# Two attention layers on one core: the place of a pair's multiplication by its softmax reciprocals in the odd block

## The chip, the cores and the metric

The kernel runs on one core of one Trainium2 chip. The metric is the device time of one execution in microseconds (us); lower is better. A core has five engines that run beside each other, each with its own queue that is worked off strictly in the order written: TensorE (PE: matmuls), VectorE (DVE), ScalarE (ACT), GpSimd (POOL) and SyncE (SP). SP and POOL here mostly issue DMAs. Engines and DMAs wait for each other through semaphores.

## The reference

The input x has 16 images of 256 channels and 32x32 points (n = 1024), all float32. Two layers of the same form follow each other, each with its own weights:

```
xn   = group_norm(x)                      # 16 groups of the last axis, mean and variance over the rest
q, k, v = W xn + b                        # 256x256 each, split in 4 heads of 64
sim  = q^T k + rel^T q                    # per head, 1024x1024; rel = rel_h + rel_w
attn = softmax(sim)
x    = x + v attn^T
```

What matters here is the end of a head: the products of v with the unnormalised exponentials are multiplied by the reciprocal of the exponentials' sum, and the result, with the bias of v, is added to x (the residual).

## The kernel before, in words

**Work and order.** A unit is one layer of one image; there are 32, interleaved so that a layer-1 unit comes four or more units after its layer-0 unit. In a unit the four heads are taken as two pairs (`pr`), and each pair in two halves of 512 queries. This gives 4 blocks a unit and 128 blocks in all. Block n of a unit has the number b = n mod 4; blocks with b = 0 and 2 (half 0) are called even, those with b = 1 and 3 (half 1) odd. The order of all instructions is written out by hand (`tc.manual_schedule`): `block(n)` issues one block, and what each engine does follows the order of the lines there. Nothing is reordered.

**A block.** For each of 8 key tiles j: DVE seeds a PSUM tile with the position term (`seed`, L346), PE adds the scores (`scores`, L382, 8 instructions of 512 columns), ACT takes the exponential into a tile `p` (L391), and DVE adds the `p` tiles up in `acc` (`add_up`, L400 and L402). PSUM has room for four such tiles, named by a ring of four tags, so a seed must wait for the exponential (or other reader) that frees its tag. The first tile of the next block is seeded and scored within the block, the next three (`seed(after, j)` for j = 1 to 3) are seeded at its end. Then PE multiplies the exponentials by v (`attend`, L416) in two stretches of 64 instructions, and ACT copies the product from PSUM to `od` (`take_out`, L477).

**Pieces for later units.** Between the scores PE also does a projection, the values or the position terms of the next unit (L265, L295, L323). Odd blocks also average the group sums of the unit after next: DVE zeroes a small PSUM tile `pm` (L202), PE adds into it (L210, in two stretches), and ACT reads it out as `neg` (L220, b = 1) or `var` (L232, b = 3). `pm` sits under the tag that the seed of tile 1 of the next block takes next, so that seed waits for this read. Two stretches of matmuls on PE are kept in order by a tiny POOL memset, the token (L166): PE's second stretch waits for the token, and POOL writes it when its queue gets there and PE's first stretch is done.

**The sums of the exponentials.** They travel by DMA. POOL issues `acc<-p` (L433, adds the last tile), then a fold of `acc` in half (L438); SP stacks a quarter of it (L452) and POOL adds the other (L457). In the second block after a pair's last one, the odd block, POOL folds the stack five times (L462: 64, 32, 16, 8 and 4 rows), each fold waiting for the landing of the one before; the first four stand in POOL's queue ahead of the token for the second stretch of `attend`. SP spreads the result into `den_all` (L470). Late in the following even block DVE takes the reciprocals (L512), SP writes them to DRAM (L514, `rd<-r`) and reads them back, broadcast over 64 partitions each, into `rden` (L519). In SP's queue both stand behind that block's L452.

**The lines of this change.** In the odd block after that (two blocks behind the folds), `before` names the pair. `normalise` (L527) multiplies `od` by `rden` in place, one DVE instruction of 128x1024. `add_residual` (L534) adds `od` and the bias of v to x, again one DVE instruction of 128x1024, and in layer 1 has SP store x (L536). `finish` (L538) is the one followed by the other; the last unit's blocks without pieces call it already. On DVE the multiplication stands behind `add_up(previous, 6)` and ahead of `seed(blk, 4)`, the residual ahead of `seed(after, 1)`:

```
        for j in range(1, 4):
            scores(blk, j)
        if before:
            normalise(*before)
...
        add_up(blk, 5)
        if before:
            add_residual(*before)
```

Of the kernel before, what the change touches and what calls it, by code (L numbers as in the profile page):

```python
# [43 lines left out]
def flat(ap):  # L44
    return ap.rearrange("p w h -> p (w h)")
# [7 lines left out]
def fast_path(ctx, tc, sh, x, layers, out, W, den_all, token, good, flag):  # L53
# [140 lines left out]
    def norm_sums(u, gs):  # L194
        if u not in reds:
            reds[u] = small.tile([P, G], F32, tag="red", name=f"red_{u}")
        for g in gs:
            of_group(u, g, AF.Identity, reds[u])
# [159 lines left out]
    def widen(u, pr):  # L358

        r = W.rel[units[u][1]][:, pr, :]  # L360
        t = gnpool.tile([P, CC, N], F32, tag="gn", name=f"wide_{u}_{pr}")[:, 0, :]
        nc.vector.tensor_tensor(
            t.rearrange("p (w y) -> p w y", y=H),
            r[:, :H].unsqueeze(1).to_broadcast([P, sh.W, H]),
            r[:, H:].unsqueeze(2).to_broadcast([P, sh.W, H]),
            ALU.add,
        )
        wide[u, pr] = t

    def scores(blk, j, tag=None):  # L370

        u, pr, half = blk
        ps = psum2(tag, f"ps_{u}_{pr}_{half}_{j}") if tag else seeds.pop((blk, j))
        columns = slice(half * HALF, (half + 1) * HALF)
        for x, c in enumerate(QUARTERS):
            for h, hs in enumerate(QUARTERS):
                j0 = j * P + x * D
                terms = [(ks[u, pr], qs[u, pr])]
                if tag:
                    terms = [(qs[u, pr], wide[u, pr])] + terms  # L380
                for i, (a, b) in enumerate(terms):
                    nc.tensor.matmul(  # L382
                        ps[c, h, :],
                        a[hs, j0 : j0 + D],
                        b[hs, columns],
                        start=bool(tag) and i == 0,
                        stop=i == len(terms) - 1,
                        skip_group_check=True,
                    )
        p = ppool.tile([P, 2, HALF], F32, tag="p", name=f"p_{u}_{pr}_{half}_{j}")  # L390
        nc.scalar.activation(p, ps, AF.Exp, bias=W.shift)  # L391
        probs[blk, j] = p

    def add_up(blk, j):
        u, pr, half = blk
        if j == 0:
            return
        if j == 1:
            accs[blk] = apool.tile([P, 2, HALF], F32, tag="acc", name=f"acc_{u}_{pr}_{half}")
            nc.vector.tensor_tensor(accs[blk], probs[blk, 0], probs[blk, 1], ALU.add)  # L400
        else:
            nc.vector.tensor_tensor(accs[blk], accs[blk], probs[blk, j], ALU.add)  # L402
# [29 lines left out]
    def add_last(blk):  # L432
        nc.gpsimd.dma_start(accs[blk], probs[blk, NT - 1], accum_op=ALU.add)  # L433
# [25 lines left out]
    def fold_stack(u, pr, rows_):  # L459

        stack = stacks[u, pr]
        nc.gpsimd.dma_start(stack[:rows_], stack[rows_ : 2 * rows_], accum_op=ALU.add)  # L462
# [61 lines left out]
    def normalise(u, pr):  # L524
        o = outs[u, pr].rearrange("p x (k e) -> p x k e", e=8)
        rden = rdens.pop((u, pr)).rearrange("p (k x e) -> p x k e", x=2, e=8)
        nc.vector.tensor_tensor(o, o, rden, ALU.mult)  # L527

    def add_residual(u, pr):

        b, l = units[u]
        xs = xt[b][:, pr, :]
        o = outs.pop((u, pr)).rearrange("p a n -> p (a n)")
        nc.vector.scalar_tensor_tensor(xs, o, W.bv[l][:, pr : pr + 1], xs, ALU.add, ALU.add)  # L534
        if l == NL - 1:
            nc.sync.dma_start(flat(out[b, pr * P : (pr + 1) * P]), xs)  # L536

    def finish(u, pr):  # L538
        normalise(u, pr)
        add_residual(u, pr)  # L540
# [75 lines left out]
    def block(n):  # L616
        blk = blocks[n]
        u, b = divmod(n, BPU)
        pr_, half = blk[1:]

        stacked = blocks[n - 3][:2] if half == 1 and n > 2 else None
        summed = blocks[n - 4][:2] if half == 0 and n > 3 else None
        before = blocks[n - 5][:2] if half == 1 and n > 4 else None
        after = blocks[n + 1] if n + 1 < len(blocks) else None
        previous = blocks[n - 1] if n > 0 else None
        one, two = u + 1 < NU, u + 2 < NU

        pieces = u + 1 < NU or b < 2
        if u + 1 == NU and b == 1:
            widen(u, 1)  # L630
        f0, f1, f2, f3 = ring
        folded = n - 1 < FOLDED
        if not pieces:
            return block_without_pieces(n, half)

        if stacked:
            fold_stack(*stacked, D)
        if previous:
            add_up(previous, 6)
            if folded:  # L640
                add_last(previous)
            else:
                add_up(previous, 7)
        for j in range(1, 4):
            scores(blk, j)
        if before:
            normalise(*before)
        (first, first_out), (second, second_out) = prepare(u, b)
        first(0)
        if b == 0 and one:  # L650
            norm_apply(u + 1, range(0, 1))
        if b == 1 and two:
            norm_sums(u + 2, range(9, 11))
        seed(blk, 4, f1)
        scores(blk, 4)
        add_up(blk, 1)
        if b == 0 and one:
            norm_apply(u + 1, range(1, 5))
        if b == 1 and two:
            norm_sums(u + 2, range(11, 12))  # L660
        if b == 2 and two:
            norm_squares(u + 2, range(0, 5))
        second(0)
        if half == 1:
            second_out()
        first.word()
        if half == 0:
            second.word()
        if stacked:
            fold_stack(*stacked, R)  # L670
        if previous and folded:
            fold(previous)
        if stacked:
            fold_stack(*stacked, R // 2)
            fold_stack(*stacked, R // 4)
        first(1)
        first_out()
        seed(blk, 5, f0)
        scores(blk, 5)
        if previous and folded:  # L680
            stack_up(previous)
        add_up(blk, 2)
        if half == 0:
            second(1)
            second_out()
        seed(blk, 6, f1)
        scores(blk, 6)
        if half == 0:
            ring[2:] = f3, f2
        seed(blk, 7, ring[2])  # L690
        scores(blk, 7)
        add_up(blk, 3)
        add_up(blk, 4)
        if summed:
            reciprocals(*summed)

        if after:
            seed(after, 0, f0)
        if n in check:
            next(checks)  # L700
        if b == 0 and one:
            norm_apply(u + 1, range(5, 9))
        if b == 0 and two:
            norm_sums(u + 2, range(0, 2))
        if b == 1 and two:
            norm_sums(u + 2, range(12, G))
        if b == 1 and one:
            norm_apply(u + 1, range(9, 11))
        if b == 2 and two:
            norm_squares(u + 2, range(5, 11))  # L710
        po = psum2(ring[3], f"po_{n}")
        values_of_p = attend(blk, po)
        values_of_p(0)
        if two and half == 1:
            mean, mean_out = (norm_mean if b == 1 else norm_var)(u + 2, zeroed(f1, f"pm_{n}"))
            mean(0)
        if after:
            scores(after, 0)
        values_of_p.word()
        if two and half == 1:  # L720
            mean(1)
        if stacked:
            fold_stack(*stacked, R // 8)
            spread_sums(*stacked)
        if previous and folded:
            fold_again(previous)
        if half == 1 and u + 3 < NU and units[u + 3][1] == 0 and u > 0 or n == 3:
            load_x(units[u + 3][0], range(pr_, pr_ + 1) if u > 0 else range(CC))
        if two and half == 1:
            mean_out()  # L730
        add_up(blk, 5)
        if before:
            add_residual(*before)
        if after:
            for j in range(1, 4):
                seed(after, j, ring[j % 3])
        if b == 0 and two:
            norm_sums(u + 2, range(2, 9))
        if b == 1 and one:
            norm_apply(u + 1, range(11, G))  # L740
        if b == 2 and two:
            norm_squares(u + 2, range(11, G))
        values_of_p(1)
        take_out(blk, po)
        pos[n] = po
# [477 lines left out]
```

## Time and profile before

| | us |
|---|---|
| median of 7 runs | 2568.03 |
| lowest and highest run | 2564.18, 2576.93 |
| the profiled execution | 2573.06 |
| its span in the profile | 2571.3 |
| one multiplication L527 (63 of them) | 1.21 to 1.23 |
| one residual L534 (63 of them) | 1.27 to 1.29 |
| `acc<-p`, issue to landing (median) | 5.2 |
| `rd<-r`, issue to landing (median) | 1.6 |
| `rden<-rd`, issue to landing (median) | 4.0 |

In the profile, a row of the timeline gives the start from the span's beginning, the duration, engine, line and operation, output and inputs, the number of merged instructions, and in brackets the idle time of the engine ahead of it and who ended it. A row of the waits gives who waited for whom, the sum, the number of times and the longest. The profiler models the ends of matmuls, so a busy PE can hide short stalls; the starts of its rows show them. "+2.3" below means 2.3 us after the first score instruction of the block on PE (the row of 24 `L382` matmuls, tiles 1 to 3).

### The profile page before, as it was taken

How to read it: one execution, taken by the hardware profiler on the slowest of the kernel's cores; microseconds unless marked ns; L12 is line 12 of the kernel's file. 1: busy time of each engine (PE TensorE's matmuls, PEld its weight loads, DVE VectorE, ACT ScalarE, POOL GpSimd, SP SyncE). 2: the span in 40 equal slices, each digit the busy share in tenths (PEclk: the TensorE clock that was granted, in tenths of full speed). 3: DMA queues.
4: the chain of work that ended last, by engine and by line, in shares of the span. 5: the costliest groups of instructions: out<-in, count | busy, mean ns of one | idle time of the engine just before them, and what ended most of it. 6: DMA issues, size and time to landing. Idle time of an engine off the chain costs nothing. (4 is left out here: it accounts for less than half of the span.)

```text
span 2571.3 us, 86058 instructions
## 1 busy us (share of the span) xinstructions
PE 2533.3 (99%) x37474; PEld 1634.6 (64%) x37474; DVE 2254.3 (88%) x2076; ACT 1957.2 (76%) x3934; POOL 833.0 (32%) x1254
## 2 busy tenths in 40 slices
PE   8999999999999999999999999999999999999997
PEld 4666766766566665666666766666655677656664
DVE  6888898988888889889888888898888888989997
ACT  6778777787777887777877777877777777787753
POOL 1233333323333333333233333333333333323320
PEclk9999999999999999999999999999999999999999
DMA  3343443444444444444444444444444444443441
GB/s 89 72 79 75 85 86 74 92 95 91 86 98 99 81 82 92 88 92 84 95 83 86 99 87 78 93 96 88 83 92 98 84 80 88 74 84 76 86 91 57
DMA packets 119538, 221.06 MB, mean 86 GB/s; under 512 B 53736, under 2 KB 55272, under 8 KB 119152
## 3 DMA queue, kind: packets, MB, share of 16 engines
q0 software_dynamic: 53568, 129.58, 30.3%
q1 hardware_dynamic: 65584, 85.90, 11.9%
q8 instruction: 295, 4.83, 0.8%
q14 instruction: 91, 0.75, 0.1%
HBM read 51.78 MB, written 17.30 MB: 27 GB/s over the span
## 5 line engine op out<-in xcount | busy, mean ns | idle before, releaser
L346 DVE TENSOR_TENSOR ps<-abt 128x1024 f32<-128x1024 f32 x1018 | 1225.7, 1227 | 233.7 <-ACT p L391 56.4
L391 ACT ACTIVATE p<-ps,shift 128x1024 f32<-128x1024 f32 x1024 | 1092.9, 1114 | 356.4 <-PE ps L382 243.3
L382 PE MATMUL ps<-q,k 64*64 64x512 f32 x8192 | 1018.8, 592 | 12.6 <-DVE ps L346 11.5
L416 PE MATMUL po<-p,v 64*64 64x256 f32 x16384 | 941.6, 376 | 0.0
L416 PEld LDWEIGHTS po<-p,v 64*64 64x64 f32 x16384 | 779.1, 133 | 183.3 <-issue 45.2
L402 DVE TENSOR_TENSOR acc<-acc,p 128x1024 f32<-128x1024 f32 x644 | 783.5, 1217 | 4.9
L382 PEld LDWEIGHTS ps<-q,k 64*64 64x64 f32 x8192 | 374.5, 133 | 356.5 <-issue 182.7
L462 POOL DMA_DIRECT2D stack<-stack x310 | 251.6, 812 | 484.4 <-DMA stack<-stack 238.3
L166 POOL MEMSET token<- 1x1 f32 x380 | 40.6, 107 | 827.0 <-PE po L416 477.2
L295 PE MATMUL pv<-Wv,xn 64*64 64x256 f32 x4096 | 250.4, 377 | 0.5 <-DVE var L876 0.3
L265 PE MATMUL pq<-xn,Wq 64*64 64x512 f32 x2048 | 250.0, 593 | 0.3 <-DVE xn L908 0.3
L265 PE MATMUL pk<-xn,Wk 64*64 64x512 f32 x2048 | 248.4, 590 | 0.0
L457 POOL DMA_DIRECT2D stack<-acc x248 | 223.6, 1090 | 40.3 <-issue 30.6
L295 PEld LDWEIGHTS pv<-Wv,xn 64*64 64x64 f32 x4096 | 190.9, 134 | 67.5 <-issue 44.2
L245 ACT ACTIVATE xn<-x,nshift,rstd 128x128 f32<-128x128 f32 x496 | 211.2, 500 | 7.5 <-POOL nshift L236 7.5
L190 ACT ACTIVATE junk<-x,neg 128x128 f32<-128x128 f32 x498 | 195.3, 401 | 0.0
L438 POOL DMA_DIRECT2D acc<-acc x124 | 102.4, 826 | 233.0 <-DMA acc<-p 223.8
L265 PEld LDWEIGHTS pq<-xn,Wq 64*64 64x64 f32 x2048 | 100.6, 134 | 120.1 <-issue 113.0
L433 POOL DMA_DIRECT2D acc<-p x124 | 131.4, 1060 | 121.6 <-DVE acc L402 107.4
L265 PEld LDWEIGHTS pk<-xn,Wk 64*64 64x64 f32 x2048 | 95.5, 134 | 105.5 <-issue 105.5
L477 ACT COPY od<-po 128x512 f32<-128x512 f32 x127 | 74.4, 586 | 113.9 <-PE po L416 113.9
L400 DVE TENSOR_TENSOR acc<-p,p 128x1024 f32<-128x1024 f32 x128 | 155.7, 1217 | 0.0
(75 smaller groups left out, 1233.7 us busy)
## 6 DMA issues: line engine op xcount, KB each, us to landing
acc<-p POOLq DMA_DIRECT2D x124, 512.0 KB, 5.2
rden<-rd SPq DMA_DIRECT2D x126, 256.0 KB, 4.0
acc<-acc POOLq DMA_DIRECT2D x124, 256.0 KB, 3.4
x<-in_x_dram SPq DMA_DIRECT2D x32, 512.0 KB, 4.3
stack<-acc SPq DMA_DIRECT2D x248, 64.0 KB, 2.1
stack<-acc POOLq DMA_DIRECT2D x248, 64.0 KB, 3.2
out_dram<-x SPq DMA_DIRECT2D x31, 512.0 KB, 3.6
stack<-stack POOLq DMA_DIRECT2D x62, 128.0 KB, 2.7
```

Source lines behind the costliest of these rows:

```text
L190: nc.scalar.activation(junk, grouped(xt[units[u][0]], g), func, accum_out=into[:, g : g + 1], **bias)
L245: nc.scalar.activation(grouped(xns[u], g), grouped(xt[units[u][0]], g), AF.Identity, bias=shift[:, g : g + 1], scale=rstd[:, g : g + 1],)
L265: yield nc.tensor.matmul(pk[c, nh, :], w[l][rs, cc, c0 : c0 + D], xns[u][rs, cc, nh * HALF : (nh + 1) * HALF], start=(t == 0 and cc == 0), ...
L295: yield nc.tensor.matmul(pv[c, a, i, :], xns[u][rs, cc, j0 : j0 + D], W.wv[l][rs, cc, :], start=(t == 0 and cc == 0 and i == 0), stop=(t = ...
L346: nc.vector.tensor_tensor(ps.rearrange("p h (w y) -> p h w y", y=H), ab[:, :, :H].unsqueeze(2).to_broadcast([P, 2, XH, H]), ab[:, :, H + h ...
L382: nc.tensor.matmul(ps[c, h, :], a[hs, j0 : j0 + D], b[hs, columns], start=bool(tag) and i == 0, stop=i == len(terms) - 1, skip_group_check ...
L391: nc.scalar.activation(p, ps, AF.Exp, bias=W.shift)
L400: nc.vector.tensor_tensor(accs[blk], probs[blk, 0], probs[blk, 1], ALU.add)
L402: nc.vector.tensor_tensor(accs[blk], accs[blk], probs[blk, j], ALU.add)
L416: yield nc.tensor.matmul(po[c, a, :QUART], vts[u][rs, j, c0 : c0 + D], p[rs, h, a * QUART : (a + 1) * QUART], start=(t == 0 and j == 0), s ...
L457: nc.gpsimd.dma_start(at, acc[R:D, h, :], accum_op=ALU.add)
L462: nc.gpsimd.dma_start(stack[:rows_], stack[rows_ : 2 * rows_], accum_op=ALU.add)
```

## The change

The multiplication leaves the front of the odd block and is made directly in front of the addition, by calling `finish` where `add_residual` was called. It does so in 61 odd blocks (block 5 to block 125). On DVE the instruction moves behind the seeds of tiles 4 to 7, five additions, the seed of the next block's tile 0, the memset of `pm` and the sixth tile's addition, and stays ahead of the seeds of the next block's tiles 1 to 3. The residual now waits on the instruction in front of it. No instruction is added or removed, no DMA is moved, and the other engines' queues keep their order.

```
@@ -643,8 +643,6 @@
                 add_up(previous, 7)
         for j in range(1, 4):
             scores(blk, j)
-        if before:
-            normalise(*before)
         (first, first_out), (second, second_out) = prepare(u, b)
         first(0)
         if b == 0 and one:
@@ -730,7 +728,7 @@
             mean_out()
         add_up(blk, 5)
         if before:
-            add_residual(*before)
+            finish(*before)
         if after:
             for j in range(1, 4):
                 seed(after, j, ring[j % 3])
```

More of the change, by code (lines that the diff above doesn't have):

```diff
@@ L645, in block @@
             scores(blk, j)
-        if before:
-            normalise(*before)
         (first, first_out), (second, second_out) = prepare(u, b)
@@ L732, in block @@
         if before:
-            add_residual(*before)
+            finish(*before)
         if after:
```

## The prediction

> **What bounds the kernel now.** I read the page's totals and the costliest groups first, then who waits on VectorE (DVE), then TensorE's (PE's) rows block by block, and last the rows of DVE and GpSimd (POOL) around the multiplication. All times are microseconds of one profiled execution.
>
> ```profile
> PE 2533.3 (99%) x37474; PEld 1634.6 (64%) x37474; DVE 2254.3 (88%) x2076; ACT 1957.2 (76%) x3934; POOL 833.0 (32%) x1254
> ...
> PE po L416 8%; PE ps L382 8%; PE pq L265 2%; PE pv L295 2%; DVE ps L346 2%; PE pk L265 2%; DMA rden<-rd 1%; DVE acc L402 1%; DMA acc<-p 1%; DMA rd<-r 1%; PE pa L323 0%; DVE acc L400 0%; POOL rstd L234 0%; DMA stack<-acc 0%; DVE od L527 0%
> ```
>
> PE is the bound. In the chain that ended last (second line) its matmuls lead, and the transfer `rden<-rd` stands there beside DVE: it is what the multiplication (L527) waits for.
>
> ```profile
> DVE od L527 <- DMA rden<-rd: 53.5, 32, 4.2
> ...
> DVE ps L346 <- ACT var L232: 39.2, 30, 2.5
> DVE ps L346 <- ACT neg L220: 36.9, 30, 2.4
> ```
>
> These are DVE's waits (total, times, longest). In 32 of 63 cases the reciprocals land late and DVE stands idle, 1.7 each. The two lower rows are 60 idle times of 1.27 each, before the first of three seeds at the end of an odd block. That is the place to which the multiplication moves.
>
> A quiet odd block, PE, DVE and ACT rows:
>
> ```profile
> 1002.09 2.75 PE L382 MATMUL ps<-q,k 64*64 64x512 f32 x24
> 1002.81 1.23 DVE L527 TENSOR_TENSOR od<-od,rden 128x1024 f32<-128x1024 f32 x1 [0.42 <-DMA rden<-rd]
> 1004.34 1.23 DVE L346 TENSOR_TENSOR ps<-abt 128x1024 f32<-128x1024 f32 x1 [0.31 <-ACT p L391]
> ...
> 1015.84 1.27 DVE L534 SCALAR_TENSOR_TENSOR x<-od,bv,x 128x1024 f32<-128x1024 f32 x1
> ...
> 1018.15 0.18 ACT L220 ACTIVATE neg<-pm 128x16 f32<-128x16 f32 x1
> ...
> 1018.36 3.50 DVE L346 TENSOR_TENSOR ps<-abt 128x1024 f32<-128x1024 f32 x3 [1.25 <-ACT neg L220]
> ...
> 1020.34 2.81 PE L382 MATMUL ps<-q,k 64*64 64x512 f32 x24
> ```
>
> A disturbed one:
>
> ```profile
> 961.71 2.81 PE L382 MATMUL ps<-q,k 64*64 64x512 f32 x24
> ...
> 964.43 1.23 DVE L527 TENSOR_TENSOR od<-od,rden 128x1024 f32<-128x1024 f32 x1 [2.38 <-DMA rden<-rd]
> ...
> 965.58 1.23 DVE L346 TENSOR_TENSOR ps<-abt 128x1024 f32<-128x1024 f32 x1
> ...
> 966.86 1.09 PE L382 MATMUL ps<-q,k 64*64 64x512 f32 x8 [0.61 <-DVE ps L346]
> ...
> 979.43 3.61 DVE L346 TENSOR_TENSOR ps<-abt 128x1024 f32<-128x1024 f32 x3 [1.09 <-ACT var L232]
> ...
> 981.32 2.86 PE L382 MATMUL ps<-q,k 64*64 64x512 f32 x24
> ```
>
> A block begins with the PE row of 24 matmuls. The quiet block lasts 1020.34 - 1002.09 = 18.25; the next odd one, from 1040.98 to 1059.26, 18.28. The disturbed one lasts 19.61: DVE waited 2.38, the fifth seed (row 965.58) came at +3.87 instead of +2.25, and PE stood still for it. Even blocks last 20.6 to 20.7 nearly everywhere. So what can be won lies in odd blocks. Lengths read from PE's rows in this way, for the 60 odd blocks that begin from 131.86 to 2460, exceed the quiet length of their kind by 30.8 together, and the last one that the change touches (2499.18) by about 0.7: **31.5**. 25 blocks are long by over 0.1, 22 of them with `rden` late.
>
> **Part 1, what the front of the block loses.** 61 multiplications of 1.22 go from the front. In a quiet block this gives nothing: the fifth seed waits for the exponential of the second tile (`ACT p`, +2.25) with or without the multiplication ahead of it, and from there to the residual DVE runs without a gap. In a disturbed block the seed falls back to +2.25 and PE's stall there goes. Were that all, 31.5 less what has other causes would be won.
>
> **Part 2, what the end of the block gains.** The multiplication now runs from +13.75 (where the residual L534 stood). Three rows at the very end of the kernel show the same pair back to back, then an independent instruction:
>
> ```profile
> 2541.51 1.22 DVE L527 TENSOR_TENSOR od<-od,rden 128x1024 f32<-128x1024 f32 x1
> 2542.76 1.28 DVE L534 SCALAR_TENSOR_TENSOR x<-od,bv,x 128x1024 f32<-128x1024 f32 x1
> 2543.96 1.22 DVE L400 TENSOR_TENSOR acc<-p,p 128x1024 f32<-128x1024 f32 x1
> ```
>
> 1.25 from product to residual, 1.20 from residual to the next: seeds can start at 13.75 + 1.25 + 1.20 = +16.20. Today they start at +16.27, when `neg` is out of PSUM (+16.38 where it is `var`). Neither waits for the multiplication: the memset of `pm` stands ahead of it, and its matmuls follow PE's own order. So the idle 1.25 covers all of it, with 0.07 to 0.14 to spare. The cover is thin. If it were gone, the third seed is what is late next: it ends at 16.27 + 3.50 = +19.77, PE wants it two tiles (1.72, from 24 matmuls in 2.57) after +18.25, so 0.2 is left (0.1 in the other kind), and everything beyond goes straight to the end. The three blocks without `neg` or `var` start their seeds at +14.95 and have 1 more to spare.
>
> The residual gets a wait on the product; behind it on DVE are only those seeds, whom PE needs as above. The output's DMA leaves SP 1.2 later at most; behind it in SP's queue stands only the next block's `stack_up`, some 10 later. The product is read out of `rden` and `od` 13 later than now, and the next tiles of these names go to other buffers (two and three). No DMA is issued at another place. `rden` landed at +4.5 at the latest, 9 ahead of the new place.
>
> The Trainium skill ("VectorE: DVE Perf Modes", The DRAIN you can't avoid) says that a semaphore between two DVE instructions costs nothing extra, since the pipe empties anyway. Here two independent seeds take 2.36 and two dependent additions 2.48, so the dependent one costs 0.12; by the page the seeds could start at about +16.08, by the rows at +16.20, and both lie under the cover. The skill also has a rule against this change ("SBUF — State Buffer", SBUF: two separate sides): a DVE instruction with two SBUF inputs and a POOL operation that reads SBUF exclude each other for a whole instruction. The residual has two SBUF inputs and stood over the same stretch, and POOL's token beside it took 0.09; were the token held to the product's end by an estimate from that rule (+15.0 instead of +14.3), 0.5 in each of 58 blocks, 27 in all, would be lost. The rows show no such hold.
>
> **Part 3, what comes up from under the wait.** PE's second stretch of products waits for a token that POOL writes, in POOL's order behind the fourth of its folding DMAs:
>
> ```profile
> 462.47 0.81 POOL L462 DMA_DIRECT2D stack<-stack  x1 [2.46 <-DMA stack<-stack]
> ...
> 463.51 0.23 PE L210 MATMUL pm<-red,avg 64*64 64x16 f32 x2 [0.72 <-POOL token L166]
> ```
>
> That fold ended at 463.28, +15.47 in its block, and PE lost 0.96 though `rden` was early. The last `pm` matmul begins 0.32 after such a fold; in quiet blocks it begins at +14.79. So a fold that ends after +14.48 costs its excess. POOL's folds wait for DMAs and not for the multiplication, hence they keep their place when the front gets faster. Reading the fold's end in the 58 blocks: it is later than +14.48 in 13 (worst +16.28 and +16.03), by **11.8** together. Most of these are blocks with late `rden`, where PE was late enough to hide it: the same slow DMAs make both late. So the excess falls from 31.5 to 11.8.
>
> **Sum.** 31.5 - 11.8 = 19.7 won. Against the profiled execution's 2573.06 (span 2571.3 and 1.8 around it): 2553.4. The median of the runs is 5.0 lower. If these 5.0 are excess too, 26.5 are left, of which the same share, 11.8 / 31.5, stays: 26.5 - 9.9 = 16.6 won, 2568.03 - 16.6 = 2551.4. I take **2552**. Bounds of the unknown: all 31.5 won gives 2541.6, none 2568.
>
> **Rivals.**
> - *The folds don't hold.* Only the token losses already visible stay, 4.1 in five blocks: 2573.06 - 27.4 = 2545.7. For it: most folds end at +12 to +13. Against: 13 fold ends read late.
> - *The wait changes its name.* If folds end 1.5 later than read in those 13 blocks, or 0.3 in all, 31.5 remains: 2563 to 2573. Against: in 41 blocks POOL waits for PE at this token, 72.1 together, 1.8 each. A half of it gives 2558 to 2563.
> - *The cover is missing, and it gets slower.* Place: the seeds after the residual. If they start a full 1.25 later, the third is 1.05 to 1.15 beyond its slack, 61 x 1.1 = 67 lost against 17 to 20 won: about 2617. It decides from a shift of 0.45 on (0.1 to 0.2 slack, and 20 / 61 = 0.33 eaten). For it: 0.07 to spare is little. Against: `neg`'s end and the seed's start are 0.03 apart, and blocks without it start the seeds 1.3 earlier.
>
> **How the numbers follow.** Forecast 0.55 (its own range 2547 to 2558); folds don't hold 0.18; half of the new wait 0.12; all of it 0.06; slower 0.09. About 0.2% (5.1) can be told from no change. Faster 0.85, same 0.06, slower 0.09. A range from 2543 to 2562 leaves out the slower case, the unchanged one and a little of the full gain.
>
> **What would show it.** Right: L527 waits for no `rden`; the seeds after the residual wait for `neg` and `var` by under 0.2 instead of 1.27, and start at +16.2 to +16.4; quiet blocks keep 18.25; PE's waits on POOL's token grow; the fifth seed starts at +2.25 everywhere. Wrong: even blocks' PE rows with idle time from `DVE ps`, quiet odd blocks over 18.4, or POOL's folds later than read.

## The result and the profile after

The changed kernel takes 2560.84 us (median of 17 runs, 2554.24 to 2566.35) against 2571.09 for the kernel before (43 runs, 2563.14 to 2580.05). The ratio is 0.9958, with a 95% interval from 0.9949 to 0.9968: it is 0.42% faster, 10.8 us by the ratio. The forecast was 2552, with 16.6 to 19.7 us won. The profiled execution took 2561.8 us with a span of 2560.0; before it was 2573.06 and 2571.3.

The page's totals of the kernel after, and the lines of the chain that ended last:

```profile
PE 2518.6 (98%) x37474; PEld 1774.1 (69%) x37474; DVE 2257.4 (88%) x2076; ACT 1955.9 (76%) x3934; POOL 833.8 (33%) x1254
...
PE po L416 7%; PE ps L382 7%; PE pv L295 2%; PE pq L265 2%; PE pk L265 2%; DMA stack<-stack 0%; DMA acc<-p 0%; PE pa L323 0%; DVE acc L402 0%; DMA stack<-acc 0%; DVE ps L346 0%; DMA rden<-rd 0%; POOL stack L462 0%; PE pm L210 0%; DMA den_all<-stack 0%
```

PE remains the bound. `rden<-rd`, 1% of the chain before, has fallen far back; `stack<-stack`, POOL's folds, is now the first transfer in it. The waits of the kernel after say the same (who waited for whom: total, times, longest):

```profile
PEld pm L210 <- POOL token L166: 46.9, 60, 3.1
...
PE pm L210 <- POOL token L166: 13.4, 14, 2.2
...
DVE ps L346 <- ACT neg L220: 8.7, 6, 2.4
...
DVE ps L346 <- ACT var L232: 3.9, 3, 2.5
...
DVE od L527 <- DMA rden<-rd: 2.6, 1, 2.6
```

The wait for `rden` went from 53.5 in 32 places to 2.6 in one (a block without pieces). DVE's idle time ahead of the seeds after the residual went from 76.1 in 60 places to 12.6 in 9: the multiplication fills it. The two rows on POOL's token have grown. The kernel before has 28.5 and 2.9 there:

```profile
PEld pm L210 <- POOL token L166: 28.5, 60, 1.6
...
PE pm L210 <- POOL token L166: 2.9, 5, 0.7
```

A quiet odd block after (b = 1), rows of PE, DVE and ACT:

```profile
1076.53 2.83 PE L382 MATMUL ps<-q,k 64*64 64x512 f32 x24
...
1078.85 1.23 DVE L346 TENSOR_TENSOR ps<-abt 128x1024 f32<-128x1024 f32 x1 [1.95 <-ACT p L391]
...
1090.35 1.21 DVE L527 TENSOR_TENSOR od<-od,rden 128x1024 f32<-128x1024 f32 x1
1091.60 1.28 DVE L534 SCALAR_TENSOR_TENSOR x<-od,bv,x 128x1024 f32<-128x1024 f32 x1
...
1092.60 0.17 ACT L220 ACTIVATE neg<-pm 128x16 f32<-128x16 f32 x1
...
1092.80 3.50 DVE L346 TENSOR_TENSOR ps<-abt 128x1024 f32<-128x1024 f32 x3
...
1094.79 2.75 PE L382 MATMUL ps<-q,k 64*64 64x512 f32 x22
```

It lasts 1094.79 - 1076.53 = 18.26; before it was 18.25. The fifth seed is at +2.32, the product at +13.82, and the three seeds at +16.27 as before, now with no idle time. In the other kind of odd block (b = 3) they start at +16.38. A block that is held up looks different. This is block 33 after, rows of PE, POOL and DVE:

```profile
682.41 2.81 PE L382 MATMUL ps<-q,k 64*64 64x512 f32 x24
...
692.72 0.81 POOL L438 DMA_DIRECT2D acc<-acc  x1 [4.23 <-DMA acc<-p]
693.25 1.09 POOL L462 DMA_DIRECT2D stack<-stack  x1
...
698.57 0.81 POOL L462 DMA_DIRECT2D stack<-stack  x1 [4.23 <-DMA stack<-stack]
699.08 0.47 POOL L166 MEMSET token<- 1x1 f32 x2
...
699.61 0.23 PE L210 MATMUL pm<-red,avg 64*64 64x16 f32 x2 [2.22 <-POOL token L166]
...
700.16 3.50 DVE L346 TENSOR_TENSOR ps<-abt 128x1024 f32<-128x1024 f32 x3 [1.42 <-ACT neg L220]
703.13 1.45 PE L382 MATMUL ps<-q,k 64*64 64x512 f32 x10
```

It lasts 20.72, 2.46 too long. The third fold is issued at 693.25 and the fourth, which waits for its landing, at 698.57. The token stands behind the fourth, and PE stops 2.22 for it. Before, the fourth fold of block 33 went out at +12.98; here it went at +16.16. (In a second profile of the kernel before, block 33 is held too, with its fourth fold at +15.53: the rows show what a held block looks like, and not that the change alone made this one late.)

**Where the time went.** "Excess" below is the sum of what the blocks 5 to 123 last beyond the quiet length of their kind, read as in the prediction. Odd blocks: 30.8 before, 20.1 after. Even blocks: 1.4 and 2.4. So 9.7 of the 11.3 between the two profiled executions lies in these blocks; of the rest, 1.3 lies ahead of them (block 5 begins at 130.59 instead of 131.86), which is not the change's doing: the second pair of profiles has it the other way round, 131.54 after and 130.51 before. Of the 20.1 left, 17.3 is PE's stop ahead of the second stretch of `attend`, in 16 blocks.

### The profile page after: what moved, and what is told of

It is laid out like the page before. It is cut to its first block, busy times and chain, and to the rows that moved or that the text cites. A ratio compares the mean times of both kernels' runs of the same rounds, so it can differ in the third digit from the quotient of the medians.

```text
span 2560.0 us, 86074 instructions
## 1 busy us (share of the span) xinstructions
PE 2518.6 (98%) x37474; PEld 1774.1 (69%) x37474; DVE 2257.4 (88%) x2076; ACT 1955.9 (76%) x3934; POOL 833.8 (33%) x1254
## 5 line engine op out<-in xcount | busy, mean ns | idle before, releaser
L416 PEld LDWEIGHTS po<-p,v 64*64 64x64 f32 x16384 | 837.9, 133 | 124.6 <-issue 42.0
L382 PEld LDWEIGHTS ps<-q,k 64*64 64x64 f32 x8192 | 421.2, 133 | 290.1 <-issue 179.4
L295 PEld LDWEIGHTS pv<-Wv,xn 64*64 64x64 f32 x4096 | 208.6, 133 | 50.9 <-issue 39.2
L245 ACT ACTIVATE xn<-x,nshift,rstd 128x128 f32<-128x128 f32 x496 | 210.9, 499 | 11.2 <-POOL nshift L236 11.2
L265 PEld LDWEIGHTS pq<-xn,Wq 64*64 64x64 f32 x2048 | 112.0, 134 | 108.6 <-issue 103.2
L265 PEld LDWEIGHTS pk<-xn,Wk 64*64 64x64 f32 x2048 | 105.9, 133 | 96.8 <-issue 94.7
```

The source lines that it names most:

```text
L245: nc.scalar.activation(grouped(xns[u], g), grouped(xt[units[u][0]], g), AF.Identity, bias=shift[:, g : g + 1], scale=rstd[:, g : g + 1],)
L265: yield nc.tensor.matmul(pk[c, nh, :], w[l][rs, cc, c0 : c0 + D], xns[u][rs, cc, nh * HALF : (nh + 1) * HALF], start=(t == 0 and cc == 0), ...
L295: yield nc.tensor.matmul(pv[c, a, i, :], xns[u][rs, cc, j0 : j0 + D], W.wv[l][rs, cc, :], start=(t == 0 and cc == 0 and i == 0), stop=(t = ...
L382: nc.tensor.matmul(ps[c, h, :], a[hs, j0 : j0 + D], b[hs, columns], start=bool(tag) and i == 0, stop=i == len(terms) - 1, skip_group_check ...
L416: yield nc.tensor.matmul(po[c, a, :QUART], vts[u][rs, j, c0 : c0 + D], p[rs, h, a * QUART : (a + 1) * QUART], start=(t == 0 and j == 0), s ...
```

## Experiments

Edits are shown against the kernel after unless said otherwise. No kernel leaves out any of the computation; three of them carry extra multiplications of a scratch tile (its allocation and first memset are not shown).

### Both kernels again

To see how far one profile's excess can be trusted, each kernel was profiled once more, with no edit.

> The changed kernel once more, for a second profile. My theory: what is left of the stall in odd blocks is PE's wait for POOL's token behind the fourth fold, and the folds end later than in the first profile of before (fourth fold ends after +14.48 in 19 of 58 blocks, 20.8 us together, against 13 and 11.8) for a systematic reason, so this profile shows again 18 to 24 us of excess length in the odd blocks, all of it at the token, and no wait for rden inside the pieces. Rival, chance of the DMAs in one execution: the fold sum falls anywhere between 8 and 24. Time 2555 to 2566.

> The kernel before once more, for a second profile. If the folds end later in the changed kernel for a systematic reason, the fourth fold's end summed over +14.48 stays at 10 to 14 here. If it was chance, it may be 8 to 24. Excess length of odd blocks 28 to 36 us, most of it at the fifth score behind a late rden. Time 2563 to 2580.

After: 2563.02 us, odd excess 19.2; fold ends beyond +14.48 sum to 18.0 in 17 blocks. Before: 2568.93 us, odd excess 28.7; fold ends 13.8 in 14 blocks. So the folds are later in the kernel after in both pairs of profiles: 20.8 against 11.8, and 18.0 against 13.8. The direction is the same in both, the size isn't (9.0 and 4.2). The third fold's way from issue to landing separates the two places of the multiplication in all profiles in which the DMAs up to that fold keep their order: 2.93 to 2.95 on average in the three with the multiplication at the front (two of the kernel before, one in the next section), 3.01 to 3.21 in the eight with it at the end or in the middle of the block. That is not one profile's chance.

### The token ahead of the fourth fold

If PE's stops come from the fourth fold's place in POOL's queue, freeing the token from it removes them. In blocks with b = 1 the fourth fold is issued behind the token:

```
         if stacked:
             fold_stack(*stacked, R // 2)
-            fold_stack(*stacked, R // 4)
+            if not (b == 1):
+                fold_stack(*stacked, R // 4)
...
         if stacked:
+            if b == 1:
+                fold_stack(*stacked, R // 4)
             fold_stack(*stacked, R // 8)
             spread_sums(*stacked)
```

> Changed kernel; in blocks with b = 1 the fourth fold is issued by POOL behind the token instead of ahead of it. Those blocks hold 15.4 us of the 20.1 us that are left in the profile of the changed kernel. My theory (the token's place in POOL's queue is what is left): these 15 go, less some 3 for the token behind the third fold and for what comes later: 2546 to 2550, ratio to before 0.990 to 0.992. Rival (PE's stall is of its own, or the DMAs are at fault wherever the token stands): unchanged, 2558 to 2563. Second rival (the later sums make the next even block wait): slower than 2563.

The same edit was made in the kernel before, with the multiplication at the front:

> Multiplication at the early place of the kernel before, and the fourth fold behind the token in blocks with b = 1 (as in the run that took 0.9903 of the time before with the late place). My theory: at the early place the wait for rden stays, since the token is not what holds it; only the 4 to 6 us that PE loses at the token in the profiles of before go. 2565 to 2570, ratio 0.9970 to 0.9990, L527 waiting for rden as often as before (about 32 times, 50 us). Rival: the token is the whole cause, and the place of the multiplication no longer matters once the token is free: ratio 0.990 to 0.992.

| multiplication | token behind the fourth fold | token ahead of it (b = 1) |
|---|---|---|
| front of the block | 1 (2571.09) | 0.9971 [0.9956, 0.9986] (2566.02) |
| end of the block | 0.9958 [0.9949, 0.9968] (2560.84) | 0.9903 [0.9883, 0.9924] (2544.75) |

With the token free, the move is worth 0.9971 - 0.9903 = 0.68% instead of 0.42%, and the two edits together give 0.97% where the sum of each alone is 0.71%. The intervals are too wide to settle that by themselves; the odd excess does. The move takes it from 30.8 to 20.1 with the token as it was, and from 23.6 (the waits for `rden` stay, 49.5 in 32 places) to 2.1 with the token free: 10.7 and 21.5. Block 5 with both edits is one in which the third fold again goes out close behind the large fold (`acc<-acc`, 0.58) and lands late, after 4.36; in the kernel after, this block lost 2.25. Its rows of PE and POOL:

```profile
130.80 2.79 PE L382 MATMUL ps<-q,k 64*64 64x512 f32 x24
...
140.86 0.81 POOL L438 DMA_DIRECT2D acc<-acc  x1 [1.70 <-DMA acc<-p]
141.44 1.03 POOL L462 DMA_DIRECT2D stack<-stack  x1
144.96 0.23 POOL L166 MEMSET token<- 1x1 f32 x2 [2.49 <-PE pm L210]
146.08 0.81 POOL L462 DMA_DIRECT2D stack<-stack  x1 [0.89 <-DMA stack<-stack]
...
149.05 2.80 PE L382 MATMUL ps<-q,k 64*64 64x512 f32 x24
```

The fourth fold goes out as late as +15.28, but POOL has written the token by then. POOL waits 2.49 for PE at the token, not PE for POOL, and the block lasts 18.25. That the rest of the gain sat behind this token, 18.0 of the 20.1, is shown. This version beats both kernels.

### The token ahead of the fourth fold in all odd blocks

```
-            fold_stack(*stacked, R // 4)
...
+            fold_stack(*stacked, R // 4)
             fold_stack(*stacked, R // 8)
```

> Changed kernel with the fourth fold behind the token in all odd blocks, not in those with b = 1 alone. Some 2 us of loss at the token were left there. In blocks with b = 3 POOL computes the next unit's deviations (about 4 us) behind the folds, so the fold that moves holds them up by some 2.5 us. My theory: the small gain is more than lost, since the scaled input comes late and the next block's sums start late: 2546 to 2565, ratio to before 0.991 to 0.998. Rival (the deviations have slack): 2541 to 2545, ratio 0.9885 to 0.990.

2570.59 us, ratio 0.9989 [0.9973, 1.0005]: nearly all of the gain is gone, worse than the expected 0.991 to 0.998. In ACT's waits of this kernel a row stands out that has 11.2, 10 times, in the kernel after:

```profile
ACT xn L245 <- POOL nshift L236: 69.2, 30, 6.1
```

In blocks with b = 3 the deviations (`rstd`, `nshift`) stand in POOL's queue behind these folds. With the fourth fold behind the token, the fifth waits there for the fourth's landing, and the deviations behind both: `nshift` starts at +5.63 of the next block (median) instead of +3.35. ACT gets it late, and the even blocks carry 23.9 of excess instead of 2.4. The odd blocks carry 13.1, nearly all of it in four blocks with b = 1 (5, 21, 29 and 85). PE's waits show another token there, which POOL now reaches late as well, ahead of the second stretch of a projection or of the values (`pk` and `pv`; the page of the kernel after has 1.5 and 1.2 for them):

```profile
PE pv L295 <- POOL token L166: 8.8, 4, 4.3
PE pk L265 <- POOL token L166: 7.2, 3, 3.6
```

The same queue serves two users, and the order that suits b = 1 doesn't suit b = 3.

### Reciprocals ahead of the stacking on SP, with the multiplication at the front

Against the kernel before: in even blocks SP's `stack_up` goes behind `rd<-r` and `rden<-rd`.

```
-        if previous and folded:
+        if previous and folded and not summed:
             stack_up(previous)
...
         if summed:
             reciprocals(*summed)
+            if previous and folded:
+                stack_up(previous)
```

> Kernel before with the multiplication at its early place, but SP issues the reciprocals' DMAs ahead of the stacking DMAs in even blocks, so rden lands some 3 us or more before the multiplication. My theory (all that the late place brings is that the multiplication no longer meets a late rden): no wait of L527 for rden, and the same as the changed kernel, 2558 to 2565, the rest at POOL's token. Rival (the place itself matters, by the idle time at the end of the block or the load at its front): over 2566, as before. Rival (stacking later makes the folds later still): 2566 to 2580 with the token's waits grown.

2699.18 us, ratio 1.0513 [1.0484, 1.0543]. The waits of this kernel, DVE's, the weight load's and PE's:

```profile
DVE od L527 <- DMA rden<-rd: 7.6, 8, 2.8
```

```profile
PEld pm L210 <- POOL token L166: 131.8, 60, 4.7
...
PE pm L210 <- POOL token L166: 79.5, 53, 3.8
```

This is far slower than any of the expectations had it. `rden` came in time, and the stack too late: the first fold goes out at +4.64 on average instead of +1.90, the fourth ends at +16.65 on average (13.43 before), the excess of the fold ends is 126.0, and that of the odd blocks 142.1. This run can't tell what the place of the multiplication is worth, since it moved something larger. It shows the price of late folds: their lateness comes back as PE's time almost one for one.

### The multiplication in the middle

On the kernel with the token free (b = 1), the product goes behind the last seed of the block, and only the residual stays at the end.

```
         scores(blk, 7)
+        if before:
+            normalise(*before)
         add_up(blk, 3)
...
         if before:
-            finish(*before)
+            add_residual(*before)
```

> Late residual, fourth fold behind the token for b = 1, and the multiplication between: behind the seed of tile 7, ahead of the additions of tiles 3 and 4, at about +7.9 of the block. rden has landed by +4.6, so no wait for it in either theory. My theory (the end of the block has an idle stretch of VectorE that just fits the multiplication, the middle has none): the seed of the next block's first tile and the memset of pm come 1.1 us later, at about +13.8, and PE, which wants them at +13.8, loses 0.1 to 0.2 in each of 58 blocks: 6 to 12 us more than the end place, ratio to before 0.992 to 0.995. Rival (any place behind rden's landing is as good): ratio 0.990 to 0.991.

2554.66 us, ratio 0.9921 [0.9904, 0.9939] against 0.9903 with the product at the end. By the two intervals alone this isn't settled; by the blocks it is: nearly every odd block is 0.14 (b = 3) or 0.19 (b = 1) longer, or more. Rows of the block that begins at 993.17:

```profile
1006.95 0.07 DVE L202 MEMSET pm<- 128x16 f32 x1
...
1007.17 0.23 PE L210 MATMUL pm<-red,avg 64*64 64x16 f32 x2
```

The memset of `pm` stands at +13.78 instead of +12.71, so PE's `pm` matmul starts at +14.00 instead of +13.83, and everything behind it follows. The end of the block has room for the product and the middle hasn't.

### More work at the front, more work at the end

On the kernel with the token free. First two scratch multiplications of 128x512 where the product used to be:

```
         for j in range(1, 4):
             scores(blk, j)
+        if before:
+            nc.vector.tensor_tensor(W.scratch[:, :HALF], W.scratch[:, :HALF], W.scratch[:, :HALF], ALU.mult)
+            nc.vector.tensor_tensor(W.scratch[:, :HALF], W.scratch[:, :HALF], W.scratch[:, :HALF], ALU.mult)
```

> Multiplication at the end, fourth fold behind the token for b = 1, and two extra multiplications of a scratch tile of 128x512 (about 1.35 us together, waiting for no DMA) where the multiplication stood before, at the front. My theory: the front costs nothing by itself, since the fifth seed waits for the exponential until +2.3 and VectorE is idle for nearly 2 us there; only the late rden made it cost. Ratio to before 0.990 to 0.9915, as without them. Rival (VectorE's load at the front is what cost time): each odd block loses up to 1.3 us, 20 to 80 us in all, ratio 0.998 or more.

2548.04 us, ratio 0.9897 [0.9880, 0.9915], the same as without them (0.9903). What the product left at the front was no gain by itself. Then one such multiplication at the end:

```
         if before:
+            nc.vector.tensor_tensor(W.scratch[:, :HALF], W.scratch[:, :HALF], W.scratch[:, :HALF], ALU.mult)
             finish(*before)
```

> Multiplication at the end, fourth fold behind the token for b = 1, and one extra multiplication of a scratch tile of 128x512 (some 0.6 us from start to start) right ahead of it. My theory: the idle stretch at the end is used up by the multiplication (first seed at +16.27 with no idle time left where neg is read, 0.01 to 0.06 where var is), so the extra 0.6 less the third seed's 0.1 to 0.2 of slack goes to PE in 58 blocks: 22 to 30 us, 2567 to 2575, ratio 0.999 to 1.002. Rival (the seeds have more slack than I read): under 10 us, ratio under 0.994.

2575.10 us, ratio 1.0004 [0.9993, 1.0014]: 26 us more than with the token free. The end of an odd block and the start of the next, DVE and PE rows:

```profile
1021.33 0.68 DVE L734 TENSOR_TENSOR scratch<-scratch 128x512 f32<-128x512 f32 x1
...
1021.93 1.22 DVE L527 TENSOR_TENSOR od<-od,rden 128x1024 f32<-128x1024 f32 x1
...
1023.18 1.28 DVE L534 SCALAR_TENSOR_TENSOR x<-od,bv,x 128x1024 f32<-128x1024 f32 x1
...
1024.39 3.50 DVE L346 TENSOR_TENSOR ps<-abt 128x1024 f32<-128x1024 f32 x3
...
1027.94 0.21 PEld L382 LDWEIGHTS ps<-q,k 64*64 64x64 f32 x8 [0.93 <-DVE ps L346]
```

The product is pushed back by 0.60, and the even blocks that follow are 0.44 longer, nearly all of them, since the third seed comes too late. That is the price from which the third rival decides, and the prediction's slack (0.07 to 0.14 ahead of the seeds, 0.1 to 0.2 behind) would have left 0.33 to 0.36 of the 0.60. So the slack was thinner than read by about 0.1. It is the third seed's that was misread: the seeds start at +16.81, 0.54 (b = 1) and 0.43 (b = 3) later than without the dose, so the idle time ahead of them was about as read (0.06 and 0.17), and behind it 0.1 and nothing were left instead of 0.2 and 0.1. A few odd blocks were also held at the token in this profile (15 and 39, which last 3.8 and 4.5 too long), which the dose doesn't explain.

### More work at the front, with the token behind the fourth fold

Why are the folds later when the multiplication is late? One theory: a stall at the front gives the chain of DMAs time, and without it the lateness of one block is carried into the next. Four such scratch multiplications at the front of the kernel after, with POOL's order left as it is, should then bring the folds back.

```
         for j in range(1, 4):
             scores(blk, j)
+        if before:
+            nc.vector.tensor_tensor(W.scratch[:, :HALF], W.scratch[:, :HALF], W.scratch[:, :HALF], ALU.mult)
...
         (first, first_out), (second, second_out) = prepare(u, b)
```

(The added line stands there four times.)

> The changed kernel (fold order as it was) with four extra multiplications of a scratch tile of 128x512 at the front of the odd block, about 2.8 us where VectorE has some 2 idle: the fifth seed comes late in every block, and PE stands still for 0.5 to 0.8 us, 61 times, as a late rden made it do in some blocks before. My theory of the size I misjudged (a stall at the front gave POOL's chain of folds time, in its own block and in those after it, so the folds read in the profile of before ended earlier than they do when that stall is gone): the fourth fold's end counted from the block's start falls from 13.8 us on average to 13.1 to 13.5, and PE's loss at the token falls from 18 to 21 us to under 8. Rival (the two profiles of before had early folds by chance or for another reason): the average stays at 13.7 to 13.9, and the loss at the token falls only by what a need that comes 0.6 later makes of the same ends, to about 10. Time 2575 to 2600.

2591.63 us (a single run). The fifth seed came at +3.0 and the quiet odd blocks were 0.47 to 0.49 longer, 28 in all. The folds did not come back: the fourth ends at +13.86 (13.81 in the kernel after). The stop at the token fell to 10.5, because PE got there 0.47 later, not because the folds were earlier. The theory fell for a short stall in every block. The stalls of the kernel before were fewer and longer (22 blocks with a late `rden`, up to 4.3), and that form was not tried.

### The third fold ahead of the large fold

Block 97 shows how a fold becomes later. POOL's rows before (the block begins at 1947.33):

```profile
1958.62 0.81 POOL L438 DMA_DIRECT2D acc<-acc  x1 [2.57 <-DMA acc<-p]
1960.18 0.78 POOL L462 DMA_DIRECT2D stack<-stack  x1 [0.75 <-DMA stack<-stack]
1962.80 0.81 POOL L462 DMA_DIRECT2D stack<-stack  x1 [1.85 <-DMA stack<-stack]
```

And after (it begins at 1939.86):

```profile
1950.36 0.81 POOL L438 DMA_DIRECT2D acc<-acc  x1 [1.99 <-DMA acc<-p]
1951.15 0.82 POOL L462 DMA_DIRECT2D stack<-stack  x1
1956.13 0.81 POOL L462 DMA_DIRECT2D stack<-stack  x1 [4.16 <-DMA stack<-stack]
```

Before, the third fold (32 KB) went out 1.56 behind the large fold `acc<-acc` (256 KB) and landed 2.35 after its issue. After, its inputs were there earlier, it went out 0.79 behind the large fold, and landed after 4.70. It started at +11.29 instead of +12.85, and yet the fourth fold started at +16.27 instead of +15.47. Over the 58 blocks of the kernel after, third folds issued within 0.9 of the large one landed after 4.07 on average, the others after 2.57 (before: 3.79 and 2.47). There are no more of the close ones than before (22 and 20; 20 and 20 in the second pair of profiles). What has grown is the number of third folds that take over 3.5: 10 to 14 of 58 in the three profiles with the multiplication at the front, 14 to 21 in the eight with it later. The edit issues the third fold ahead of the large one in odd blocks, and leaves the token where it is:

```
+        if stacked:
+            fold_stack(*stacked, R // 2)
         if previous and folded:
             fold(previous)
         if stacked:
-            fold_stack(*stacked, R // 2)
             fold_stack(*stacked, R // 4)
```

> Changed kernel, fourth fold ahead of the token as it was; in odd blocks POOL issues the third fold of the stack ahead of the 256 KB fold of acc instead of behind it. In ten profiles so far the third fold lands 3.6 to 4.2 us after its issue where it goes out within 0.9 us behind the 256 KB fold (20 to 24 of 58 blocks) and 2.4 to 2.7 us after it elsewhere; with the multiplication late, five or six blocks have changed from the short to the long kind. My theory (that the transfer behind the big one makes the fourth fold, and the token, late): the third fold lands in 2.2 to 2.8 us everywhere, PE's loss at the token falls from 18 to 21 us to under 6, time 2545 to 2552, ratio to before 0.9895 to 0.993. Rival (the third fold is slow in these blocks because of other traffic, whatever stands ahead of it): losses at the token stay over 12, 2554 or more.

2556.01 us, ratio 0.990 [0.987, 0.993], with the kernel before at 2577.93 beside it. The third fold landed after 2.63 on average (3.14 in the kernel after), the stop at the token fell from 17.3 to 7.8 and the odd excess from 20.1 to 8.3. POOL's rows of block 33, which begins at 680.79:

```profile
691.21 0.79 POOL L462 DMA_DIRECT2D stack<-stack  x1 [4.19 <-DMA stack<-stack]
691.72 1.13 POOL L438 DMA_DIRECT2D acc<-acc  x1
693.91 0.81 POOL L462 DMA_DIRECT2D stack<-stack  x1 [1.06 <-DMA stack<-stack]
694.95 0.23 POOL L166 MEMSET token<- 1x1 f32 x2 [0.23 <-PE pm L210]
```

The fourth fold goes out at +13.12 instead of +16.16. The token loss and the time are a little above the expectation (under 6, and 2552 at most), and the even blocks lose 8.2, part of it again through `nshift`. But half of the loss at the token goes by exchanging two DMAs in one queue, so the order behind the large fold is shown to cost that half. The ratio makes this run look better than it is, since the kernel before was slow beside it: the profiled executions of the kernel after and of this one are 5.0 apart (2561.8 and 2556.84).

### Both orders

> Both changes of POOL's order together: third fold ahead of the 256 KB fold, and the fourth behind the token for b = 1. Alone the second gave a ratio of 0.9903 and left some 2 us of loss at the token in odd blocks. If the first does what I think, some 1 to 2 us more go: 2542 to 2546, ratio 0.9885 to 0.9905. Rival (the big fold, now 1.5 us later, makes the later DMAs and the deviations late): as much or more is lost in even blocks, ratio 0.991 or more.

The third fold ahead of the large one, and the token ahead of the fourth fold where b = 1: 2546.86 us, ratio 0.9875 [0.9845, 0.9904]. Against the token alone (0.9903 [0.9883, 0.9924], 2544.75 us) it can't be told apart; the 1 to 2 us more that were expected don't show. The odd excess is 2.3 against 2.1: with the token free, an earlier third fold has nothing left to give.

## Why the prediction was right, and where its size was off

- **Part 1, the front.** Right. No block with pieces waits for `rden`, the fifth seed stands at +2.25 to +2.34 in every odd block, and quiet blocks gained nothing. The doses confirm the reason: about 1.35 of extra work at the front costs nothing once the token is free.
- **Part 2, the end.** Right in all that the profile can show: seeds at +16.27 and +16.38, idle time ahead of them 0.00 to 0.06, quiet blocks at 18.26 and 18.28. The cover fits, and just so: 0.60 more would have cost 0.44 a block, where the prediction's slack leaves 0.33 to 0.36. The third rival had the right place and, by 0.1, too low a price; its case didn't come about. No hold of POOL by the product can be seen either: the quiet blocks kept their lengths within 0.01. But they don't test the rule of the Trainium skill ("SBUF — State Buffer", SBUF: two separate sides) by which the prediction worked out an estimated 0.5 in each block. That rule speaks of a POOL operation that reads SBUF, and the token is a memset with no input; the prediction applied it where it doesn't hold.
- **Part 3, what comes up from under the wait.** The mechanism was right: PE's stop at POOL's token took the place of the stalls at the front. The step that failed is "hence they keep their place when the front gets faster", and with it the term **11.8**. A fold end beyond +14.48 costs what the prediction said (20.8 by the fold ends of the kernel after, 20.1 by its odd blocks), but the fold ends moved; "POOL's folds later than read" was among the prediction's own signs of being wrong. The fourth fold goes out at +13.01 on average instead of +12.62. Of these 0.39, 0.21 are the third fold's longer way (3.14 from issue to landing instead of 2.93) and 0.15 a later first fold; the second pair of profiles has the 0.21 again (3.16 and 2.95) and not the 0.15 (1.96 and 1.98); there the fourth fold goes out 0.12 later (12.97 and 12.85). In 18 and 20 of 58 blocks the third fold takes over 3.5, where it was 10 and 14. In the first pair these blocks hold 15.7 of the 20.8 (7.1 of the 11.8 before); the rest, 5.1 and 4.6, stayed. The profile from which 11.8 was read was also a low one: the second profile of the same kernel gives 13.8.
- **The sum.** In blocks 5 to 123 the odd excess fell by 10.7 (30.8 to 20.1) where 11.8 left over would have made it 19.0; even blocks took back 1.0. The profiled execution gained 11.3, the ratio says 10.8. This one term is 8.3 of the 8.4 by which the gain of the profiled execution fell short of 19.7; the even blocks and the 1.3 at the start nearly cancel. The step from the profiled execution to the median (5.0, taken as excess) rested on seven runs. With the 43 runs it is 2.0, and the same working gives 2552.6, so it isn't where the miss lies. The rival "the wait changes its name" had a price for its half, 2558 to 2563, and that is where the time lies. The stated range, 2543 to 2562, holds 2560.84 because it was drawn wide enough for this rival; the forecast's own, 2547 to 2558, doesn't hold it. That is width and not insight. The rival's other condition was mis-sized: folds 0.3 later in all 58 blocks make 15.9 of the 11.8, not 31.5. "The folds don't hold" (2545.7) was off by 15. The argument against the rival, 41 blocks in which POOL waits for PE at the token, read slack from quiet and disturbed blocks alike: the slack of 1.8 was an average, and a landing of 4 or 5 instead of 2.5 uses it up.
- **What stays open.** That the third fold takes longer with the late multiplication is shown, and that its place behind the large fold costs about half of the loss at the token. Why a move on DVE makes `acc<-p` or the second fold land at other times is not settled. In block 97 the third fold goes out within 0.9 behind the large one in seven of the eight profiles with the multiplication later and in none of the three with it at the front, hence it isn't noise alone. A later `acc<-p` alone (block 33) can do it too, and that came in both profiles of the kernel after and in one of the kernel before. The run with work at the front speaks against a carry of lateness from block to block, but it tried only a short stall in every block.

## What to carry to other kernels

When a wait is removed, look at the queue that comes next and ask how close its transfers stand to the deadline, block by block: a threshold turned a shift of 0.4 in the mean into 8 us of loss, and their place read from the old trace isn't kept. A small write that releases the bottleneck (here a token of 0.09) should not stand behind a DMA that waits for another's landing, unless something later in the same queue needs that DMA first. Work can move into a gap of known length if both ends of the gap are read to 0.1: 0.60 more than the moved instruction cost 0.44 in nearly every block behind it.

## What the runs showed of the hardware

- A DMA of 32 KB that is issued on POOL's queue within 0.9 us behind one of 256 KB landed 1.0 to 1.6 us later on average than otherwise in eleven profiles (4.07 against 2.57 after, 3.79 against 2.47 before); issued 0.5 ahead of it, it landed after 2.63 on average.
- The later place of that small DMA is decided by when its own input lands: an earlier input made the whole chain later by 0.8 in block 97.
- PE's busy share (99% before, 98% after) says nothing of 10 us: the stops at the front of the odd blocks were seen in the starts of its rows, and the sum of the block lengths gave 9.7 of the 11.3 between the profiled executions.
